# The causal mask of the second attention: an addition by VectorE in PSUM in place of a product by TensorE

## The chip, the cores and the metric

The kernel runs on one core of one Trainium2 chip. Its metric is the device time of one execution in microseconds (us); the time of a version is the median of several executions. A profiled execution gives in addition the record of every instruction on five engines: TensorE (PE; its weight loads are listed as PEld), VectorE (DVE), ScalarE (ACT), GpSimd (POOL) and SyncE (SP).

## The reference

The reference is a chain of eight layers (four attentions or mixers, four feed-forward layers) over an input of 8 sequences x 256 tokens x 256 features in fp32, each followed by a residual and a layer norm. The change touches the second attention, cut here to its core:

```python
def _L1_attn_ref(x, Wq, Wk, Wv, Wo, gq, gk):        # 16 heads of 128
    q = _rmsnorm((x @ Wq.T).reshape(B, T, H, hd), gq)
    k = _rmsnorm((x @ Wk.T).reshape(B, T, H, hd), gk)
    v = (x @ Wv.T).reshape(B, T, H, hd)
    ...
    scores = jnp.einsum('bhqd,bhkd->bhqk', q, k) * scale
    mask = k_idx > q_idx
    scores = jnp.where(mask[None, None], -jnp.inf, scores)
    attn = jax.nn.softmax(scores.astype(jnp.float32), axis=-1)
    out = jnp.einsum('bhqk,bhkd->bhqd', attn, v)
    return out.transpose(0, 2, 1, 3).reshape(B, T, H * hd) @ Wo.T
```

A query sees the keys up to its own position. With 256 tokens and tiles of 128, the first 128 queries need the first 128 keys alone, and the last 128 queries need all 256; only the blocks of 128 x 128 on the diagonal are masked element by element.

## The kernel before

The layers run one after another; the second attention (`attn1`, from L1256) takes the stretch from about 530 to 1280 us of the profiled execution. Its work is cut into 32 units: 8 sequences x 4 groups of four heads. A loop of 34 turns (L1436 and after) runs three stages of the work beside each other: in turn n, unit n makes its keys, queries and values (back = 0), unit n-1 its scores and softmax (back = 1), unit n-2 its output (back = 2). The order of all instructions in a turn is written out by hand there, each engine takes its own in that order, and no scheduler moves them.

The steps, by name and line:

- `keys` and `queries` project tokens on four heads (L1282, 512 columns), square them on ScalarE (L1290) and sum the squares on VectorE (L1291). `scaled` scales the keys on VectorE (L1304); ScalarE copies the queries (L1315). `turned` transposes both on TensorE (L1329); VectorE copies the turned queries (L1334), ScalarE the turned keys (L1336).
- `values` projects the values (L1282 again); VectorE copies one half, ScalarE the other (L1324).
- `scores` is called three times per unit: once for the first 128 queries of all four heads (`qc` 0, four products of 128 columns), and twice for the last 128 queries, two heads each (`qc` 1, two products of 256 columns). Each call fills one PSUM bank of 512 columns (tag "s", two banks). After the products of q and k (L1349), one more product adds the mask to the diagonal blocks: identity times `maskA`, the mask in bf16 for four heads side by side (L1353). VectorE then takes the negative row maxima over the whole bank (L1358) and scales them (L1360), and ScalarE makes the exponentials, one instruction per head (L1362), with their sums.
- `weights` turns the sums into reciprocals on VectorE (L1370) and scales the exponentials on GpSimd (L1372).
- `turn_weights` transposes the weights of two heads (L1382, L1384) and copies them to `pT` with the helper `copy` (L114), which gives one copy to VectorE (L118) and the next to ScalarE (L120), in turn.
- `weigh` multiplies the values by `pT` (L1396, L1399) and copies the result to `attT`, with `copy` again.
- `finish`, once per sequence, multiplies `attT` by Wo (L1410).
- In the first turns, the last of the layer before is done beside this one (L1174 to L1195).

An fp32 product has two records on TensorE, a bf16 product one. `tri` (128 x 256, fp32) is in SBUF from the start: its second half holds 0 on and below the diagonal and -1e30 above it; `maskA` is made from it (L97).

The calls around the scores in one turn stand in this order:

```python
at(0, "scaled", 0)
at(1, "scores", 0, 0)
at(2, "turn_weights", 2)
at(0, "queries", 0)
at(0, "scaled", 1)
step()
at(2, "weigh", 2)
```

Of the kernel before, what the change touches and what calls it, by code (L numbers as in the profile page):

```python
# [15 lines left out]
ALU = mybir.AluOpType  # L16
AX = mybir.AxisListType

P = 128
# [20 lines left out]
class Model:  # L40
# [1215 lines left out]
    def attn1(self, w, act, beside, then, start=False):  # L1256
# [4 lines left out]
        nc = self.nc  # L1261
# [6 lines left out]
        class Unit:  # L1268
# [69 lines left out]
            def scores(u, qc, h0):  # L1338
                n = 2 - qc
                n *= 2  # L1340
                nk = (qc + 1) * P
                if h0 == 0:
                    if qc == 0:
                        u.p, u.sums = {}, {}
                    u.p[qc] = act.tile([P, 4, nk], F32, tag=f"p{qc}", name="p")
                    u.sums[qc] = self.small.tile([P, 4], F32, tag="sums", name="sums")
                sc = self.ps("s").rearrange("p (j k) -> p j k", k=nk)
                for j in range(n):
                    nc.tensor.matmul(  # L1349
                        sc[:, j, :], u.qT[:, h0 + j, qc * P : (qc + 1) * P],  # L1350
                        u.kT[:, h0 + j, 0:nk], start=(j == 0), stop=False,
                    )
                nc.tensor.matmul(  # L1353
                    sc[:, :, nk - P :], self.identb, self.maskA[:, :n, :],
                    start=False, stop=True,
                )
                nm = self.small.tile([P, 4], F32, tag="nm", name="nm")
                nc.vector.tensor_reduce(nm[:, :n], sc, AX.X, ALU.max, negate=True)  # L1358
                r = u.rq[:, 4 * qc + h0 : 4 * qc + h0 + n]
                nc.vector.tensor_tensor(nm[:, :n], nm[:, :n], r, ALU.mult)  # L1360
                for j in range(n):
                    nc.scalar.activation(  # L1362
                        u.p[qc][:, h0 + j, :], sc[:, j, :], AF.Exp,
                        bias=nm[:, j : j + 1], scale=r[:, j : j + 1],
                        accum_out=u.sums[qc][:, h0 + j : h0 + j + 1],
                    )
# [904 lines left out]
```

## Time and profile before

| | |
|---|---|
| median of 3 runs | 2552.52 us (2549.58 to 2555.33) |
| profiled execution, its own time | 2540.15 us |
| its span | 2538.4 us |
| busy over the span | PE 88%, DVE 56%, ACT 41%, POOL 36% |
| granted TensorE clock, mean over the span | 0.945 |
| instructions in the span | 36327 |

The span runs from the first to the last instruction; 1.75 us of the execution's own time lie around it. "Busy" counts the time in which an engine has at least one record. Records of TensorE overlap, because products are pipelined, and their ends are modelled. In the views below, "idle before" is the time that an engine had no record ahead of an instruction, with the instruction that released it.

### The profile page before, as it was taken

How to read it: one execution, taken by the hardware profiler on the slowest of the kernel's cores; microseconds unless marked ns; L12 is line 12 of the kernel's file. 1: busy time of each engine (PE TensorE's matmuls, PEld its weight loads, DVE VectorE, ACT ScalarE, POOL GpSimd, SP SyncE). 2: the span in 40 equal slices, each digit the busy share in tenths (PEclk: the TensorE clock that was granted, in tenths of full speed). 3: DMA queues.
4: the chain of work that ended last, by engine and by line, in shares of the span. 5: the costliest groups of instructions: out<-in, count | busy, mean ns of one | idle time of the engine just before them, and what ended most of it. 6: DMA issues, size and time to landing. Idle time of an engine off the chain costs nothing. (4 is left out here: it accounts for less than half of the span.)

```text
span 2538.4 us, 36327 instructions
## 1 busy us (share of the span) xinstructions
PE 2225.3 (88%) x12016; PEld 1510.7 (60%) x12016; DVE 1432.9 (56%) x3597; ACT 1044.6 (41%) x3001; POOL 916.3 (36%) x1725
## 2 busy tenths in 40 slices
PE   8998979989999999999999999998887787668990
PEld 4554678856666666666664555555555555457780
DVE  3655276755445444445455444646788878745363
ACT  1223345544445345345342112221576656644450
POOL 1222325344334333333213221000466656833555
PEclk9998999999999999999999999999998978789995
DMA  5000321110000100000070011001000000145673
GB/s 158 1 1 1 118 70 46 34 42 4 3 4 3 52 1 1 1 1 1 15 261 1 0 50 50 2 0 63 40 1 1 1 1 22 42 123 166 210 216 95
DMA packets 92309, 120.76 MB, mean 48 GB/s; under 512 B 9757, under 2 KB 79582, under 8 KB 91102
## 3 DMA queue, kind: packets, MB, share of 16 engines
q1 hardware_dynamic: 82270, 95.75, 11.6%
q0 software_dynamic: 8192, 21.11, 2.8%
q8 instruction: 100, 1.64, 0.3%
q10 hardware_dynamic: 1664, 1.57, 0.2%
q14 instruction: 83, 0.68, 0.1%
HBM read 67.53 MB, written 50.88 MB: 47 GB/s over the span
## 5 line engine op out<-in xcount | busy, mean ns | idle before, releaser
L1372 POOL TENSOR_SCALAR p<-p,rs 128x128 f32<-128x128 f32 (+1 forms) x256 | 104.2, 424 | 293.7 <-DVE rs L1370 289.4
L1362 ACT ACTIVATE p<-ps_s,nm,rq 128x128 f32<-128x128 f32 (+1 forms) x256 | 128.0, 507 | 151.1 <-DVE nm L1360 151.1
L146 POOL TENSOR_SCALAR rsq<-bnmv 128x2 f32<-128x2 f32 x64 | 13.6, 212 | 454.0 <-DVE bnmv L184 446.4
L1290 ACT ACTIVATE sq<-ps_a 128x512 f32<-128x512 f32 x126 | 76.0, 603 | 225.8 <-PE ps_a L1282 225.5
L647 ACT ACTIVATE e<-ps_a,nm 128x128 f32<-128x128 f32 (+1 forms) x256 | 105.9, 435 | 107.7 <-DVE nm L644 93.3
L1291 DVE TENSOR_REDUCE ssk<-sq 128x4 f32<-128x512 f32 x64 | 43.8, 686 | 172.3 <-ACT sq L1290 172.3
L689 POOL TENSOR_SCALAR v<-e,r,nmd 128x128 f32<-128x128 f32 (+1 forms) x256 | 134.7, 537 | 10.0
L1282 PE MATMUL ps_a<-w_a_wq,xT 128*128 128x512 f32 x256 | 121.5, 597 | 11.8 <-DVE k L1304 9.2
L1282 PE MATMUL ps_a<-w_a_wv,xT 128*128 128x512 f32 x256 | 122.2, 600 | 2.1 <-ACT q L1315 2.1
L706 PE MATMUL ps_t<-ident,v 128*128 128x128 f32 x384 | 68.7, 316 | 61.4 <-DVE qT L585 30.1
L1962 PE MATMUL ps_a<-w_f_gup,xTg 128*128 x504 | 112.2, 347 | 10.8 <-DVE xTg L1956 4.2
L681 DVE SCALAR_TENSOR_TENSOR e<-e,c 128x128 f32<-128x128 f32 (+1 forms) x256 | 105.9, 463 | 24.9 <-POOL c L668 24.8
L1291 DVE TENSOR_REDUCE ssq<-sq 128x4 f32<-128x512 f32 x64 | 43.9, 686 | 130.5 <-ACT sq L1290 130.5
L1282 PE MATMUL ps_a<-w_a_wk,xT 128*128 128x512 f32 x248 | 116.5, 593 | 0.0
L1410 PE MATMUL ps_o<-w_a_wo,attT 128*128 128x256 f32 x512 | 111.8, 379 | 0.0
L647 ACT ACTIVATE e<-ps_s,nm 128x128 f32<-128x128 f32 (+1 forms) x256 | 106.8, 451 | 0.0
L1410 PEld LDWEIGHTS ps_o<-w_a_wo,attT 128*128 128x128 f32 x512 | 96.7, 190 | 12.8
L1146 DVE SCALAR_TENSOR_TENSOR yg<-ps_t,xg,yg 128x128 f32<-128x128 f32 x266 | 93.1, 350 | 12.5 <-PE ps_t L1135 3.6
L1349 PE MATMUL ps_s<-kT,qT 128*128 128x256 f32 (+1 forms) x512 | 99.5, 327 | 0.0
L706 PEld LDWEIGHTS ps_t<-ident,v 128*128 128x128 f32 x384 | 49.9, 162 | 81.1 <-issue 31.3
L1396 PE MATMUL ps_o<-pT,V 128*128 128x256 f32 x256 | 79.5, 392 | 19.3 <-ACT pT L120 19.2
L1962 PEld LDWEIGHTS ps_a<-w_f_gup,xTg 128*128 128x128 f32 x504 | 83.0, 198 | 21.3 <-ACT yg L1992 10.7
(403 smaller groups left out, 6116.0 us busy)
## 6 DMA issues: line engine op xcount, KB each, us to landing
rows<-zero SPq DMA_DIRECT2D x42, 384.0 KB, 4.4
xg<-rows SPq DMA_DIRECT2D x42, 384.0 KB, 3.4
outs<-yg SPq DMA_DIRECT2D x42, 384.0 KB, 3.6
w_f_gup<-in_f_gup SPq DMA_DIRECT2D x8, 768.0 KB, 9.7
w_f_w<-in_f_w SPq DMA_DIRECT2D x8, 512.0 KB, 5.4
w_f_down<-in_f_down SPq DMA_DIRECT2D x8, 384.0 KB, 9.0
w_f_up<-in_f_up SPq DMA_DIRECT2D x5, 512.0 KB
lrows<-zero SPq DMA_DIRECT2D x12, 204.0 KB, 5.7
```

The lines of the kernel that those rows point to most:

```text
L647: nc.scalar.activation(e[:, s, j * nk : (j + 1) * nk], sc[s][:, j, :], AF.Exp, bias=nm[:, s, j : j + 1], scale=1.0, accum_out=sums[:, s, j ...
L681: nc.vector.scalar_tensor_tensor(d[:, s, h, :], u.e[:, s, h, 1, :], u.c[:, s, h : h + 1], d[:, s, h, :], ALU.mult, ALU.add,)
L689: nc.gpsimd.tensor_scalar(u.v[:, s, h, :], d[:, s, h, :], u.r[:, s, h, 0:1], nm[:, s, h : h + 1], ALU.mult, ALU.add,)
L706: nc.tensor.transpose(ps[:, s, c, :], x, self.ident)
L1146: nc.vector.scalar_tensor_tensor(acc[j], y, c, acc[j], ALU.mult, ALU.add)
L1282: nc.tensor.matmul(ps, self.xt(u.b, t, c), w[which][:, c, u.cols], start=(c == 0), stop=(c == 1),)
L1291: nc.vector.tensor_reduce(out, sq, AX.X, ALU.add)
L1349: nc.tensor.matmul(sc[:, j, :], u.qT[:, h0 + j, qc * P : (qc + 1) * P], u.kT[:, h0 + j, 0:nk], start=(j == 0), stop=False,)
L1362: nc.scalar.activation(u.p[qc][:, h0 + j, :], sc[:, j, :], AF.Exp, bias=nm[:, j : j + 1], scale=r[:, j : j + 1], accum_out=u.sums[qc][:, h ...
L1372: nc.gpsimd.tensor_scalar(u.p[qc][:, j, :], u.p[qc][:, j, :], ri[:, j : j + 1], 1.0, ALU.mult, ALU.mult,)
L1410: nc.tensor.matmul(y[:, t, :], attTs[b][:, h, t * P : (t + 1) * P], w["wo"][:, h, :], start=(h == 0), stop=(h == 15),)
L1962: nc.tensor.matmul(ps, xT[j][:, c, :], w["gup"][:, bass.ds(er[j], 1), c, :].rearrange("p o f -> p (o f)"), start=(c == 0), stop=(c == 1),)
```

## The change

The last product of q and k now closes the bank's sum, the product with the mask is gone, and VectorE adds the mask instead: it reads the diagonal blocks of the bank, adds the second half of `tri`, repeated over the heads, and writes them back to the same place in PSUM. The reduction that follows reads the bank as before. On TensorE 96 products and the 96 weight loads that belong to them go away (32 of 512 columns, 64 of 256), on VectorE 96 instructions come in, each right before its reduction (32 of 512 elements per partition, 64 of 256). ScalarE, GpSimd and SyncE have the same instructions in the same order. `maskA` stays in use in the other attentions.

```diff
                 for j in range(n):
                     nc.tensor.matmul(
                         sc[:, j, :], u.qT[:, h0 + j, qc * P : (qc + 1) * P],
-                        u.kT[:, h0 + j, 0:nk], start=(j == 0), stop=False,
-                    )
-                nc.tensor.matmul(
-                    sc[:, :, nk - P :], self.identb, self.maskA[:, :n, :],
-                    start=False, stop=True,
+                        u.kT[:, h0 + j, 0:nk], start=(j == 0), stop=(j == n - 1),
+                    )
+                diag = sc[:, :, nk - P :]
+                nc.vector.tensor_tensor(
+                    diag, diag, self.tri[:, P:].unsqueeze(1).to_broadcast([P, n, P]), ALU.add
                 )
                 nm = self.small.tile([P, 4], F32, tag="nm", name="nm")
                 nc.vector.tensor_reduce(nm[:, :n], sc, AX.X, ALU.max, negate=True)
```

## The prediction

> **What bounds the kernel now.** I read the page first (TensorE busy for 88% of the span, VectorE 56%), then the busy time by stretches. The scores of the second attention lie between 530 and 1280 us:
>
> ```profile
> core 0: us, PE busy (x) PEld busy (x) DVE busy (x) ACT busy (x) POOL busy (x), PEclk, DMA share, GB/s
> ...
> 530.00:1280.00 750.00, 716.67 (x3250) 485.64 (x3249) 351.40 (x730) 339.40 (x891) 261.46 (x479) 1.00 0.04 12
> ```
>
> The columns are the stretch, its length, and the busy us of each engine with its instructions. TensorE has work for 96% of the stage at clock 1.00, VectorE for 47%. That looks as if any product taken off TensorE were time won. So I looked next at whom TensorE waits for, at the line of the product that weighs V (L1396):
>
> ```profile
>   ACT pT L120: 51.9, 62
>   issue: 15.6, 65
>   DVE pT L118: 5.7, 14
> ```
>
> Each line is a releaser, us in total, times. 62 is 32 waits of weight loads and 30 of products: in nearly each of the stage's 34 turns TensorE stands still once until ScalarE has copied a pT. The timeline tells why that copy is late. One turn, others left out:
>
> ```profile
> 711.67 1.06 PE L1349 MATMUL ps_s<-kT,qT 128*128 128x128 f32 x8
> ...
> 712.05 0.68 DVE L1304 TENSOR_TENSOR k<-ps_a,rk 128x512 f32<-128x512 f32 x1
> ...
> 712.56 0.38 PE L1353 MATMUL ps_s<-maskA,identb 128*128 128x512 bf16 x1
> ...
> 712.77 0.27 PE L1382 MATMUL ps_t<-ident,p 128*128 128x128 f32 x1
> ...
> 712.98 0.69 DVE L1358 TENSOR_REDUCE nm<-ps_s 128x4 f32<-128x512 f32 x1 [0.24 <-PE ps_s L1353]
> ...
> 713.70 0.16 DVE L1360 TENSOR_TENSOR nm<-nm,rq 128x4 f32<-128x4 f32 x1
> ...
> 713.98 0.46 ACT L1362 ACTIVATE p<-ps_s,nm,rq 128x128 f32<-128x128 f32 x1 [1.53 <-DVE nm L1360]
> ...
> 715.74 0.48 ACT L120 COPY pT<-ps_t 128x384 f32<-128x384 f32 x1
> ...
> 716.27 0.70 PE L1396 MATMUL ps_o<-pT,V 128*128 128x256 f32 x2 [0.20 <-ACT pT L120]
> ```
>
> The columns are start, duration, engine, line. The copy stands on ScalarE behind the four exponentials of this turn's first scores, and these wait for the maxima, which wait for the masked scores. So a **chain** from scores to L1396 runs through the very place that the change touches, and TensorE idles at its end, though it looks busy. A second kind of turn idles longer, with the reduction bound by VectorE's own queue:
>
> ```profile
> 980.71 0.68 DVE L1304 TENSOR_TENSOR k<-ps_a,rk 128x512 f32<-128x512 f32 x1
> 980.79 0.38 PE L1353 MATMUL ps_s<-maskA,identb 128*128 128x512 bf16 x1
> ...
> 981.30 0.68 DVE L1358 TENSOR_REDUCE nm<-ps_s 128x4 f32<-128x512 f32 x1
> ...
> 984.59 0.70 PE L1396 MATMUL ps_o<-pT,V 128*128 128x256 f32 x2 [1.05 <-ACT pT L120]
> ```
>
> Here the reduction starts 0.59 us after L1304, as any VectorE instruction of 512 elements lets the next one start about 0.6 us later; it shows no wait for the mask. Reading the 32 units one after another, the reduction waits for the mask in 13 (kind A) and follows another VectorE instruction without a gap in 19 (kind B).
>
> **What the Trainium skill says.** "Perfetto Trace Analysis", Identifying the Most-Contended Engine, says that matmul busy share does not measure distance to the limit. The trace agrees: counting a product of 512 fp32 columns as the 0.43 us between starts (256: 0.215, 128: 0.11), TensorE idles about 46 us here, against the 33 us that the busy row leaves. "VectorE: DVE Perf Modes", The TRN2 errata, prices an fp32 tensor_tensor at (N+151)/0.96 ns: 691 for 512 elements, 424 for 256. L1304, of this form, took 680. The same page, The DRAIN you can't avoid, says that a read after a write on VectorE needs a semaphore. The trace shows its price: L1358 to its reader L1360 is 0.72 us, 0.04 more than the record.
>
> **The change part by part.** Per unit, three scores groups: one of four heads (first queries) and two of two heads (second queries).
>
> *Removed:* 96 products and 96 weight loads of identb.
>
> ```profile
> L1353 PE MATMUL ps_s<-maskA,identb 128*128 128x256 bf16 x64 | 17.4, 273 | 0.0
> L1353 PE MATMUL ps_s<-maskA,identb 128*128 128x512 bf16 x32 | 12.1, 379 | 0.0
> L1304 DVE TENSOR_TENSOR k<-ps_a,rk 128x512 f32<-128x512 f32 x62 | 42.1, 680 | 0.0
> ```
>
> 273 and 379 ns are latencies; what TensorE gets back is the distance to the next product: 0.22 us for 512 columns (712.56 to 712.77) and 0.11 for 256. That is 0.22 + 2 x 0.11 = 0.44 us per unit, 14 us over 32 units. The identb loads (98 ns) ran beside the products before them: nothing. The stop flag on the last scores product: nothing.
>
> *Added:* 96 VectorE additions, whose reader (L1358) is next in the queue. For 512 elements 0.68 us like L1304, plus the 0.04 of a dependent reader: 0.72. For 2 x 128, 0.41 by the slope between 384 elements (550 ns) and 512 (687), plus 0.04: 0.45. No row of before shows VectorE writing PSUM; from below I bound the step by 0.60 (no wait for its own result), from above by 0.85 (0.1 more for a write to PSUM, a guess of mine). I take 0.72: L1304 reads the same memory, L1358 hands over in the same way. The mask operand is repeated over heads and costs no element more.
>
> *Behind the additions on VectorE* stand L1358 and L1360, then copies of pT, V, qT and the reciprocal; ScalarE's exponentials wait for L1360.
>
> *First-query group.* Kind A: before, from the first scores product to the mask 0.89, to the reduction 0.42 more (0.22 the product, 0.20 until VectorE sees it), 1.31. After: 0.89 + 0.20 + 0.72 = 1.81, so 0.50 later. Kind B: VectorE was the last to be ready, so the whole 0.72. Exponentials, pT copy and L1396 move by as much; the time saved on the product before it turns into a longer stand. What is late next: nothing new, since ScalarE's squares and q copy (L1290, L1315), for which later products wait, follow the same copy.
>
> *Second-query groups.* The two products give 2 x 0.11 = 0.22 back, because from L1396 to the next scores the turn is TensorE's: its idle there is next to nothing. The two additions delay the reduction by 0.45 - 0.11 = 0.34. Cover: at 990.50 to 991.49 VectorE waits 0.83 for V's product, and qT's second copy (995.05) follows a wait of 1.11 for TensorE, while the exponentials that feed the reciprocal at 995.66 end some 0.9 earlier. So nothing; without that cover, up to 0.34 twice per unit.
>
> *Sum:* A 13 x (0.50 - 0.22) = 3.6; B 19 x (0.72 - 0.22) = 9.5; together **+13.1 us**. The profiled execution took 2540.15 (span 2538.4), so 2553.3; it stands 12 us under the median 2552.52 of the three runs, for which I predict 2565.6. With the bounds of 0.60 and 0.85 in place of 0.72: +9.3 and +17.3.
>
> ScalarE, POOL and SP keep their instructions and order.
>
> **Rivals.** *TensorE's stream decides (faster).* If the chain had slack, the 14 us come back: 2538.5. For it speak 96% busy and VectorE at 47%; against it the waits at L1396, one in nearly each turn, and the reduction at the head of each. It decides only if the addition adds less to the chain than 0.44 per unit in the mean, that is, if it cost under about 0.5 us instead of 0.72.
>
> *Even.* The stand at L1396 absorbs part of it, because the TensorE records there are modelled ends and the idle is smaller than I read, or the added 0.6 us of kind B is taken from VectorE's waits. About +3: 2555.5.
>
> *A second chain opens (slower still).* The second-query additions make the reciprocal (L1370) late, so POOL's scaling L1372, for which the loads of L1384 wait already (5.5 us over 19 waits in the list of waits from 600 to 1200 us, without TensorE idling yet). Another 0.34 per unit, 11 us: +24, 2576.5. Against it the 0.9 us of cover.
>
> *The change doesn't do what it says:* the instruction lists show the 96 additions in place of the 96 products, so I give this nothing.
>
> **Numbers.** A difference within 0.2% (5.1 us) can't be told from none. Chain: 0.74; second chain: 0.08; even: 0.09; TensorE's stream: 0.09. Faster 0.09, same 0.10 (the even case and a tail of the chain), slower 0.81. The range runs from 2556 (chain at its cheapest, less a run's spread of 3 us) to 2576 (chain at its dearest with that spread, up to the second chain).
>
> **What would show it.** Right: additions of 512 near 0.68 us, L1358 in kind A some 1.8 us after the first scores product, L1396's wait for ACT pT grown by about 0.5 to 0.7 per unit, TensorE busy down by some 14 us while the stage grows by 13. Wrong: waits at L1396 that do not grow, a new wait at L1384, or an addition much shorter or longer than L1304.

## The result, and the profile after

The changed kernel took 2573.47 us (median of 6 runs, 2571.4 to 2575.41), the kernel before 2552.26 us beside it (6 runs): 21.2 us more, ratio 1.0082 with a 95% interval of 1.0070 to 1.0094. The forecast was 13.1 us more, with a range of 2556 to 2576 us.

The loss lies in the stage of the second attention. I measure the stage from the start of the first scores product (L1349) to the start of the last product of Wo (L1410): 531.5 to 1297.4 us in the profiled execution before, 534.5 to 1321.9 after, so 765.9 and 787.4 us, **21.5 us more**. (The whole spans of these two executions differ by 34.5 us. I don't read the other 13 as the change's: outside the stage they took 1772.5 and 1785.5 us, and in the experiments below that time was 1767 to 1772 us in all profiled executions of the first set and 1782 to 1786 in all of the two others, whatever the kernel. The profiled execution of before, 2540.15 us, is also 9 us under the fastest of the six executions above. It is the only profile of before, so every stage below is compared with it across sets; where that matters, the medians beside each other decide.)

The price of the addition, in the groups of the profile after (partitions x elements, count, busy us, mean ns, idle before):

```profile
L1354 DVE TENSOR_TENSOR ps_s<-ps_s,tri 128x256 f32<-128x256 f32 x64 | 27.7, 432 | 5.2 <-PE ps_s L1349 5.0
L1354 DVE TENSOR_TENSOR ps_s<-ps_s,tri 128x512 f32<-128x512 f32 x32 | 22.2, 694 | 4.8 <-PE ps_s L1349 4.5
L1358 DVE TENSOR_REDUCE nm<-ps_s 128x4 f32<-128x512 f32 x32 | 22.1, 692 | 1.1
```

694 ns against the 680 taken from L1304, 432 against the estimate of 410: in these two forms writing to PSUM costs hardly more. The reduction, which waited 7.6 us for the product before, now follows the addition with 1.1 us of idle in all. A kind A turn in the timeline after:

```profile
720.09 1.06 PE L1349 MATMUL ps_s<-kT,qT 128*128 128x128 f32 x8
...
720.47 0.68 DVE L1304 TENSOR_TENSOR k<-ps_a,rk 128x512 f32<-128x512 f32 x1
...
721.18 0.70 DVE L1354 TENSOR_TENSOR ps_s<-ps_s,tri 128x512 f32<-128x512 f32 x1
...
721.92 0.69 DVE L1358 TENSOR_REDUCE nm<-ps_s 128x4 f32<-128x512 f32 x1
...
722.92 0.46 ACT L1362 ACTIVATE p<-ps_s,nm,rq 128x128 f32<-128x128 f32 x1 [2.05 <-DVE nm L1360]
...
724.68 0.48 ACT L120 COPY pT<-ps_t 128x384 f32<-128x384 f32 x1
...
725.21 0.70 PE L1396 MATMUL ps_o<-pT,V 128*128 128x256 f32 x2 [0.90 <-ACT pT L120]
```

From the first scores product to the reduction it is 1.83 us (1.31 before, 1.81 forecast), to the second pair of L1396 5.12 (4.60 before). A kind B turn:

```profile
993.59 0.68 DVE L1304 TENSOR_TENSOR k<-ps_a,rk 128x512 f32<-128x512 f32 x1
...
994.19 0.69 DVE L1354 TENSOR_TENSOR ps_s<-ps_s,tri 128x512 f32<-128x512 f32 x1
...
994.91 0.69 DVE L1358 TENSOR_REDUCE nm<-ps_s 128x4 f32<-128x512 f32 x1
...
998.21 0.70 PE L1396 MATMUL ps_o<-pT,V 128*128 128x256 f32 x2 [1.90 <-ACT pT L120]
```

L1304 to the reduction is 1.32 us where it was 0.59: the whole addition, as forecast. The idle ahead of L1396 went from 1.05 to 1.90 us. Undisturbed turns got longer by 0.29 us in kind A (19.62 to 19.91 between two first-query reductions) and by 0.51 in kind B (20.36 to 20.87). The forecast was 0.28 and 0.50. Whom L1396 waits for, in the profile after (us, times):

```profile
  ACT pT L120: 91.2, 62
  DVE pT L118: 14.8, 27
  issue: 11.5, 37
```

Weight loads and products together wait 91.2 us for ScalarE's copy, 51.9 before; the same wait is counted once for the load and once for the product. The products alone wait 38.9 us where it was 19.2, which is 0.6 us more per unit. The weight loads of L1384, where the prediction looked for a second chain, wait for GpSimd 7.3 us over 25 times, 8.0 over 25 before. So the mechanism of the prediction is there, turn by turn. One sign named in it came out otherwise: TensorE was to be busy for 14 us less, and by its records it is busy for 728.5 us of the stage after 732.6, 4 less.

But four turns, those that end with the first-query reductions at 702, 1075, 1214 and 1273 us, are 1.98 to 2.19 us longer than before instead of 0.3 or 0.5. This is what happens ahead of the first of them, in the busy time by stretches of the profile after (length, then busy us and instructions of PE, PEld, DVE, ACT, POOL, and the granted clock):

```profile
680.50:683.90 3.40, 1.50 (x8) 1.19 (x8) 0.98 (x3) 3.03 (x11) 0.00 (x0) 1.00 0.00 0
683.90:687.30 3.40, 3.40 (x10) 2.10 (x9) 1.20 (x4) 1.27 (x2) 1.43 (x4) 0.50 0.00 0
```

TensorE has records in only 1.50 of the first 3.4 us, since it waits for the pT copy, and in the next 3.4 us its **granted clock is 0.50**. The profile before has no such stretch in the stage. The four of after lie at 683.9, 1055.9, 1195.9 and 1253.9 us, 3.41 us each. At half clock 3.41 us do the work of 1.7, so I estimate their cost as 4 x 1.7 = 6.8 us. The turns agree: taking off the 0.3 or 0.5 of their kind leaves 1.7 us in each of the four. It also lengthens TensorE's records, and so explains up to 6.8 of the 10 us by which its busy time fell short of the sign; the rest I have not followed up.

### The profile page after: what moved, and what is told of

Its sections match the earlier page's. It is cut to its first block, busy times and chain, and to the rows that moved or that the text cites. A ratio compares the mean times of both kernels' runs of the same rounds, so it can differ in the third digit from the quotient of the medians.

```text
span 2572.9 us, 36207 instructions
## 1 busy us (share of the span) xinstructions
PE 2224.2 (86%) x11896; PEld 1508.3 (59%) x11920; DVE 1480.7 (58%) x3693; ACT 1042.0 (41%) x3001; POOL 918.9 (36%) x1725
## 3 DMA queue, kind: packets, MB, share of 16 engines
q1 hardware_dynamic: 82270, 95.75, 11.6%
## 5 line engine op out<-in xcount | busy, mean ns | idle before, releaser
L146 POOL TENSOR_SCALAR rsq<-bnmv 128x2 f32<-128x2 f32 x64 | 13.7, 214 | 453.1 <-DVE bnmv L184 444.9
L1282 PE MATMUL ps_a<-w_a_wq,xT 128*128 128x512 f32 x256 | 125.0, 611 | 14.7 <-DVE k L1304 11.4
L1396 PE MATMUL ps_o<-pT,V 128*128 128x256 f32 x256 | 82.3, 403 | 40.4 <-ACT pT L120 38.9
L1410 PE MATMUL ps_o<-w_a_wo,attT 128*128 128x256 f32 x512 | 111.8, 379 | 0.0
L1410 PEld LDWEIGHTS ps_o<-w_a_wo,attT 128*128 128x128 f32 x512 | 96.7, 190 | 12.8
L1349 PE MATMUL ps_s<-kT,qT 128*128 128x256 f32 (+1 forms) x512 | 99.4, 327 | 0.0
```

Of the source, the lines that this page charges most:

```text
L1282: nc.tensor.matmul(ps, self.xt(u.b, t, c), w[which][:, c, u.cols], start=(c == 0), stop=(c == 1),)
L1349: nc.tensor.matmul(sc[:, j, :], u.qT[:, h0 + j, qc * P : (qc + 1) * P], u.kT[:, h0 + j, 0:nk], start=(j == 0), stop=(j == n - 1),)
L1410: nc.tensor.matmul(y[:, t, :], attTs[b][:, h, t * P : (t + 1) * P], w["wo"][:, h, :], start=(h == 0), stop=(h == 15),)
```

## The experiments

Three sets of kernels, each set on one chip beside the kernel before. "Stage" is measured as above in the profiled execution, against the 765.9 of before; "net" has 1.7 us taken off for each 3.41 us of half clock in it, by the estimate above. "Half clock" tells of the one profiled execution of each kernel. Ratios are to before, with a 95% interval, from 5 rounds.

| kernel | median, before beside it (us) | ratio | stage | half clock | net, against before |
|---|---|---|---|---|---|
| product first | 2533.8, 2538.9 | 0.9977 (0.9970 to 0.9985) | 760.0 | none | -5.9 |
| addition first | 2563.7, 2538.9 | 1.0093 (1.0078 to 1.0109) | 796.7 | 20.5 us | +20.5 |
| filler of four | 2556.1, 2538.9 | 1.0068 (1.0055 to 1.0082) | 781.8 | none | +15.9 |
| changed, VectorE copies | 2528.7, 2538.9 | 0.9960 (0.9946 to 0.9973) | 755.6 | none | -10.3 |
| changed, again | 2572.5, 2550.6 | 1.0092 (1.0076 to 1.0108) | 787.4 | 13.7 us | +14.7 |
| before, VectorE copies | 2530.7, 2550.6 | 0.9916 (0.9898 to 0.9934) | 741.9 | none | -24.0 |
| product first, VectorE copies | 2526.2, 2550.6 | 0.9896 (0.9879 to 0.9913) | 736.1 | none | -29.8 |
| second masks twice | 2578.0, 2550.6 | 1.0107 (1.0090 to 1.0124) | 784.0 | 3.4 us | +16.4 |
| changed, third time | 2578.3, 2552.9 | 1.0106 (1.0090 to 1.0123) | 791.1 | 23.9 us | +13.3 |
| filler of two | 2566.7, 2552.9 | 1.0060 (1.0044 to 1.0076) | 781.1 | none | +15.2 |
| first masks twice | 2603.1, 2552.9 | 1.0195 (1.0174 to 1.0216) | 819.5 | 34.1 us | +36.6 |

In the cuts of the edits below, white space that only moved is left out, and so is the stop flag of the last scores product, which stays open where a mask product follows.

**Product for the first-query groups, addition for the second.**

```diff
+                if qc == 0:
+                    nc.tensor.matmul(
+                        diag, self.identb, self.maskA[:, :n, :], start=False, stop=True
+                    )
+                else:
                     nc.vector.tensor_tensor(
                         diag, diag, self.tri[:, P:].unsqueeze(1).to_broadcast([P, n, P]), ALU.add
                     )
```

> The mask of the first-query groups is added by the product again, that of the second-query groups stays with VectorE. Chain theory (only the first-query mask lies on the chain to L1396; the second-query additions are covered): 64 products of 256 columns are saved, 64 x 0.11 = 7 us under the kernel before, and no half-clock stretch in the stage. Second-chain theory (the second-query additions make the reciprocal late): not faster, 0 to 15 us over before.

The stage is 5.9 us shorter, the ratio puts it at 4 to 8 us. The waits of TensorE's products in the stage (us, times, longest) are, in the kernel before, in the changed one, and in this one, where L1402 is L1396 of before:

```profile
PE ps_o L1396 <- ACT pT L120: 19.2, 30, 1.2
PE ps_o L1396 <- ACT pT L120: 38.9, 30, 1.9
PE ps_o L1402 <- ACT pT L120: 19.2, 30, 1.2
```

The wait is back at the value of the kernel before to the digit. The second-query half of the change is a gain of the size that TensorE's stream gives, and does not lengthen this stand (a stand is a stretch in which TensorE waits); the loss is in the first-query half.

**The reverse**, with `if qc == 1` in the same place.

> The reverse: VectorE adds the mask of the first-query groups, the product that of the second-query groups. Chain theory with the clock (long stands at L1396 end in stretches of half clock): 13 x 0.50 + 19 x 0.72 = 20 us of chain and some 7 us of half clock, 27 us over before, thus slower than the changed kernel by about 7. Second-chain theory (what the change cost over the predicted 13 us comes from the second-query additions): those are gone, so about 20 over before and no slower than the changed kernel.

```profile
PE ps_o L1402 <- ACT pT L120: 38.9, 30, 1.9
```

The wait is that of the changed kernel, and net of half clock the stage is 20.5 us longer, the 20 of the chain. The profiled execution had six stretches of half clock and was the longest of its four; the median is 24.8 us over before, between the two expectations. That median alone would not decide between them, but with the second-query additions gone the loss is as large as ever.

**The second-query masks added twice**, to ask for the cover itself.

```diff
-                nc.vector.tensor_tensor(
-                    diag, diag, self.tri[:, P:].unsqueeze(1).to_broadcast([P, n, P]), ALU.add
-                )
+                for _ in range(2 if qc == 1 else 1):
+                    nc.vector.tensor_tensor(
+                        diag, diag, self.tri[:, P:].unsqueeze(1).to_broadcast([P, n, P]), ALU.add
+                    )
```

> The changed kernel with the mask of the second-query groups added twice (masked scores become -2e30 instead of -1e30, which leaves the same weights). 64 more VectorE instructions, 64 x 0.45 = 29 us of VectorE time. Chain theory: covered (each reduction is 0.34 + 0.45 = 0.79 later than before, the cover read from the trace is 0.8 to 0.9), so within 3 us of the changed kernel, apart from stretches of half clock. Second-chain theory: up to 0.45 to 0.9 us per unit, 14 to 29 us slower than the changed kernel.

The wait of TensorE's products (L1397 is L1396):

```profile
PE ps_o L1397 <- ACT pT L120: 38.9, 30, 1.9
```

It is that of the changed kernel, and the net stage is 1.7 us longer for 29 us more of VectorE's time. In this execution the cover held. It was the fastest of its six, though, 9 us under their median. The medians of this kernel and of the changed one in the same set differ by 5.4 us, more than the 3 expected and with overlapping intervals, and the profiled execution had one stretch of half clock where the other had four, so I don't split that difference further. It is well under the 14 to 29 us of a second chain.

**The first-query masks added twice**, with `2 if qc == 0`.

> The changed kernel with the mask of the first-query groups added twice (-2e30 where masked, which leaves the same weights). 32 more VectorE instructions of 512 elements. Chain theory: each adds its full 0.72 us to the chain, 32 x 0.72 = 23 us over the changed kernel; kind B then stands 2.7 us, so more windows have over 2.06 us of idle: some 6 to 8 stretches of half clock in place of 4, 3 to 7 us more; together 26 to 30 over the changed kernel. Second-chain theory: the first-query chain has no more share than predicted 0.41 (13.1 us over 32): 13 us.

24.8 us over the changed kernel of the set by the medians; by the stages 28.4 in all, 23.3 net, which is the 32 x 0.72 = 23 of the chain. The medians are a little under the 26 to 30 us expected, and nearly twice the 13 of the second chain. Ten windows of half clock, 34.1 us, stand where there were seven, 23.9.

**A filler in the stand.** Four products into the bank that `weigh` is about to fill:

```diff
                 o = self.ps("o").rearrange("p (h t) -> p h t", h=2)
+                if h0 == 2:
+                    for _ in range(4):
+                        nc.tensor.matmul(
+                            o.rearrange("p h t -> p (h t)"), self.identb,
+                            self.maskA.rearrange("p j k -> p (j k)"), start=True, stop=True,
+                        )
```

> The changed kernel, with four products of identity and mask (512 columns, 0.86 us together) into the bank of weigh, ahead of L1396 for the last two heads of each unit; their result is overwritten. They fit into the stands (1.13 us in kind A, 1.9 in kind B), so they cost no time by themselves. Clock theory: no 3.4 us window has 2 us of idle any more, the four stretches of half clock in this stage are gone, about 7 us less than the changed kernel, 14 over before. If the half-clock stretches are not set by the stands: unchanged, 21 over before. If TensorE's stream bounds: 28 us slower than the changed kernel.

There is no half clock in the stage, and the kernel is 17.2 us over before, between the 14 expected if the stands set the clock and the 21 if they don't. As this set had no changed kernel beside it, I repeated the question with half the filler, `range(2)`, beside a changed kernel:

> The changed kernel as it is, as the measure for the two others of this set on one chip: 20 to 22 us over before, about 4 stretches of half clock in the stage.

> The filler with two products (0.43 us) in place of four. Reading of the traces so far: a window of 3.4 us is followed by half clock where TensorE idles 2.06 us or more of it; the largest idle of one window was 2.17 us, so 0.43 us less suffices. Clock theory: no stretch of half clock in the stage, 5 to 7 us less than the changed kernel of this set. Rival (half clock comes and goes by itself): about 4 stretches and the same time.

The stage as one stretch, first in the changed kernel of that set, then with the filler (the last columns are the granted clock, the share of the DMA engines, GB/s):

```profile
534.10:1325.20 791.10, 732.93 (x3237) 499.31 (x3236) 399.53 (x827) 337.57 (x892) 260.69 (x478) 0.98 0.06 20
```

```profile
536.30:1317.40 781.10, 733.66 (x3300) 499.68 (x3299) 399.46 (x827) 337.72 (x892) 261.63 (x478) 1.00 0.06 20
```

63 more records on TensorE, the clock back at 1.00, and the stage 10 us shorter; the medians differ by 11.6 us, and the intervals of the two ratios don't overlap. That is more than the 5 to 7 us expected: the changed kernel had seven windows of half clock this time, and was 25.4 us over before instead of 20 to 22. The mean clock of all executions of the two kernels, 0.941 to 0.943 and 0.943 to 0.947, goes the same way. More work on TensorE made the kernel faster. So the half clock comes from the stands.

**The copies moved off the chain.** In the changed kernel, both pT copies of the last two heads go to VectorE:

```diff
-                    self.copy(pT, pt[:, : 3 * P])
+                    if h0 == 2:
+                        nc.vector.tensor_copy(pT, pt[:, : 3 * P])
+                    else:
+                        self.copy(pT, pt[:, : 3 * P])
```

> The changed kernel, with both pT copies for the last two heads of a unit on VectorE, so that no pT copy stands behind the exponentials on ScalarE. Chain theory: L1396 no longer waits for ScalarE; what is late next is the q copy L1315 behind the exponentials, so kind A gains about 0.3 and kind B about 1.0 us per unit, 23 us, and the half-clock stretches (7 us) go: about 30 under the changed kernel, 9 under before. If the wait at L1396 only stands in for TensorE's own stream: unchanged.

10.2 us under before. The wait for ScalarE's copy at L1396 is gone from TensorE's products (two waits of 1.1 us in all for VectorE's copies are left there), and what is late next is what was named, with the keys beside it:

```profile
PE ps_a L1282 <- ACT q L1315: 15.9, 29, 3.3
PE ps_a L1282 <- DVE k L1304: 11.4, 10, 1.6
```

Net of half clock the stage is at -10.3 where the changed kernel of the other sets had +13.3 and +14.7: 24 to 25 us for the 23 read off the timeline.

**The same edit in the kernel before, and with the product kept for the first masks alone.**

> The kernel before, mask by product everywhere, with both pT copies for the last two heads of a unit on VectorE. Chain theory: the stands at L1396 go (0.47 us in kind A, 1.21 in kind B, less 0.1 for the q copy that is late next): 13 x 0.4 + 19 x 1.1 = 26 us under before. If the stands are modelled ends and not real: no change.

> Product for the first-query mask, addition for the second-query masks, and both pT copies for the last two heads on VectorE: the two gains together. Chain theory: 26 us and 7 us, 33 under before, the fastest of all. If the second-query additions lose their cover once the stands are gone: no faster than the kernel before with the copies alone (26).

Stages of the two:

```profile
536.10:1278.00 741.90, 726.89 (x3301) 500.58 (x3332) 366.98 (x763) 326.19 (x860) 260.78 (x478) 1.00 0.06 20
```

```profile
533.30:1269.40 736.10, 720.03 (x3236) 497.52 (x3267) 391.96 (x827) 324.13 (x860) 261.70 (x478) 1.00 0.06 21
```

24.0 and 29.8 us under the stage before. The medians say 19.9 and 24.3 us, less than the stages by 4 to 5, which I have not followed up, and less than the 26 and 33 expected. The last one beats both the kernel before and the changed one, at 0.9896 of before. Against the kernel before with the copies moved, its stage is 5.8 us shorter, as with the copies in place (5.9), but the intervals of the two ratios overlap.

**The changed kernel once more** was run beside these, to see whether the size of the loss belongs to one chip:

> The changed kernel as it is, timed beside the others of this set on one chip. Chain and clock theory: 13 us of chain and about 7 of half clock, 20 us over before; by the first pair of traces 2 to 6 stretches of half clock in the stage. If the 8 us over the prediction came from that one chip alone: about 13.

It is 21.9 us over before, with four stretches of half clock in the stage again, and the third set, on another chip, has 25.4 us. So the size does not belong to one chip.

## Why the prediction was right, and where its size was off

- *The bound.* Right. The 96% of the stage in which TensorE was busy was not the limit; the chain from scores to L1396 was. Moving the copies showed it, and the wait moved where it was said to move.
- *Removed.* Right: 0.22 and 0.11 us per product, given back only in the second-query groups. The kernel with the product for the first masks keeps just that half and gains 5.9 us in the stage for the 7 counted.
- *Added.* Right: 0.694 us for the estimate of 0.68, 0.72 to 0.74 to the reader.
- *First-query group.* Right in both kinds to 0.02 us (1.83 for 1.81; 0.73 for 0.72).
- *Second-query groups at nothing.* Right within the turns; doubling them left the wait at L1396 as it was. It does not hold at the end of the stage: behind the last first-query reduction, where no next unit stands beside the work, the last reciprocal (L1370) starts after 9.19 us instead of 8.66, and the stage ends 0.7 us later. There the second chain of the prediction opens, once.
- *Sum.* Here is the error. 13.1 us were forecast, and the stage grew by 21.5. The distances between the first-query reductions, without the four turns' half clock, add up to 13.2 us. The stretch ahead of the first of them gave 0.7 us, the whole of an addition, since no second-query product lies in it whose saving could be set against it. The stretch behind the last gave the other 0.7. The rest, 4 x 1.7 = 6.8 us, is a term that the sum did not have: it took the granted clock of 1.00 as fixed and a stand as worth its own length.
- *Rivals.* TensorE's stream as the sole bound was wrong. The cost below which it was to decide, 0.5 us, was too high as well: of the 0.44 us per unit the sum counts only the 0.22 of the second-query groups as won, and it comes out even at 9.9 / 32 = 0.31 us. The second chain was wrong but for the 0.7 us at the end. The even case fell with the ratio.
- *Range.* That it held was in part luck. The chain alone, at its dearest and with a run's spread, gives 2552.5 + 17.3 + 3 = 2572.8 us, and the measured 2573.47 lies above that; the top of 2576 was drawn for the second chain, and the 21 us lie near its +24 for another reason. At the lower end the text's own working gives 2558.8, not 2556.

## What to carry to other kernels

Before moving work from a busy engine to an idle one, look for a wait that recurs on the busy engine and follow it back: the same mask was worth 4 to 8 us on VectorE where VectorE's work was covered, and cost 20 us, and some half clock besides, where a chain runs through it. An engine that looks 96% busy can still be waiting once in every turn. And price a stand on TensorE by what it does to the clock as well, not by its length alone.

## What the runs showed of the hardware that I had not expected

The half-clock stretches of one execution lie on a grid of 3.41 us (683.9 to 1055.9 is 109 steps, to 1195.9 another 41, to 1253.9 another 17). I cut the stage of all thirteen profiled executions on that grid, between 545 and 1265 us, and added TensorE's idle in each window. Idle is counted here by the distances between starts, as in the prediction; by the modelled ends of the records it is 0.2 to 0.3 us less (2.17 us in the window at 680.5, where the records above leave 1.90). Of the windows at full clock, each of the 21 with 2.13 us or more of idle was followed by a window of half clock; none with less than 2.05 us was; between these it went both ways. So in this stage stands of 1.3 us (the longest at L1396 before) never cost clock, and one of 2.06 us (kind B after) does where one window of the grid holds it nearly whole, together with some idle more. This fits that the turns hit differ from run to run. All of these windows are of this one loop; whether it is idle time as such that counts, these runs don't show.

The Trainium skill, "TensorE: Matmul & The Clock Gate", What's actually happening, tells of two states, half clock "after ≥1 idle window (~3.4µs)", and of a window that runs free of the program. The window and its free running agree with these traces. But no window needed to be idle as a whole: 2.13 of 3.41 us, some 62%, were enough in each case here.
